# Closing a pair of sequences behind the second down product, and sending its rows one iteration later

## The chip, the cores and the metric

The kernel runs on one core of a Trainium2 chip. A core has five engines, each with its own in-order stream of instructions: TensorE (PE in the profile; PEld is its weight load), VectorE (DVE), ScalarE (ACT), GpSimd (POOL) and SyncE (SP, which here only issues DMAs and reads registers). They wait for each other through semaphores. The metric is the device time of one execution in microseconds, given as the median of several runs. Beside it stands one profiled execution, whose trace has the start and the duration of every instruction.

## The reference: what is computed

The model has two layers on 32 sequences of 128 tokens with 512 features. Each layer adds a feed-forward part, applied to a mixture-of-experts part, to its input:

```python
x = x + ffn0(cond0(x, ...))      # cond0: shared expert + 2 of 8 routed experts
x = x + ffn1(cond1(x, ...))      # cond1: hashed experts;  ffn1: a recurrent scan
```

The change touches only the end of the first line and the entry of the second. `ffn0` chooses one of 8 experts for each whole sequence (its own expert) from the sequence's last token, and then computes for all its tokens

```python
h = gelu(hidden @ w1 + b1)               # 512 -> 1024
reasoned = h @ w2 + b2                   # 1024 -> 512
out = hidden + 0.3 * (reasoned @ Wo + bo)
```

`cond1` first mixes each token with the one before it in its sequence, with two sets of coefficients:

```python
xk = x + (xprev - x) * time_maa_k        # goes to the hashed experts
xr = x + (xprev - x) * time_maa_r        # goes to r = sigmoid(xr @ w_recept.T)
```

The stage that is changed hands on three things for every sequence: the new `x` itself, the rows of `xk`, and the rows of `xr @ w_recept.T`.

## The kernel before, in words

All products are made in a split format: each float32 operand is stored as a rounded high part and the remainder, and a product is three matmuls (high x high, high x low, low x high). The helper `split` makes the two parts with one ScalarE cast and one VectorE subtraction; the helper `mm3` makes the matmuls. In the profile every matmul of a split product therefore has line L64, every cast L56 and every subtraction L57, and one reads by the names of the tiles.

The stage of the sequences' own experts is one loop (line 1115), over `b` from -1 to 32. It is software-pipelined: iteration `b` makes the first products of sequence `b+1`, the second products of sequence `b`, and the closing work of earlier sequences. The sequences were sorted by expert beforehand in two parts (0 to 23 and 24 to 31), so that neighbours mostly share their weights.

- `up(b, half)` (line 981): half of the 512-to-1024 product, 12 matmuls of 512 columns, tile `pu`; ScalarE copies it out as `ue`.
- `bend(b, half)` (line 988): four transposes (tile `pt`), four ScalarE gelus (tile `hf`), then a split into `hb`, which the down product reads.
- `down(b, half)` (line 1000): half of the 1024-to-512 product, 12 matmuls, tile `po`. After half b ScalarE copies the sum out as `ps`.
- `turn_r(b)` (line 1012): four transposes of `ps` (tile `pr`), then four times a ScalarE step and a VectorE step that write the high and low part of `rT`. Each ScalarE step here waits for the VectorE step before it.
- `close(c)` (line 1029) for the pair of sequences `2c` and `2c+1`: 48 matmuls of 256 columns against `Wo` (tile `pb`), then on VectorE the new `x1` (line 1058), the difference `dx` (L1041), `xk` (four instructions, L1043). GpSimd writes the first column of `x1` (L1034); SyncE stores `x1`, two DMAs.
- `fetch_xh(c)` (line 967): two DMAs that load the next pair's addend. `mix_r(c)` (line 1075): four VectorE instructions that turn `dx` into the other mix (L1079), then a split into `xr` (ScalarE cast, VectorE subtraction).
- `send_k(b)` (line 1085): four transposes of `xk` (tile `ptB`), a ScalarE copy into `rows`, one store. `send_v(b)` (line 1095): 12 matmuls of `xr` against `w_recept` (tile `pv`), a ScalarE copy into `r`, one store. `rows` and `r` share two buffers.
- `used()` (line 1110) stands behind each of the four weight products. It holds the split of the next weight of that kind (`split_w`, line 839: two casts and two subtractions of 128 x 1024), inside a branch that ScalarE and VectorE take only if the next sequence has another expert; then GpSimd gathers the weight three places further on. By the casts in the trace the branches are taken for sequences 7, 16, 24 and 27.

The transposes `pt`, `pr` and `ptB` share two PSUM banks (pool `ps_t`), `pb` and `pv` share three.

Within a stretch between two such branches the framework's scheduler may reorder instructions; across a branch no engine's instructions move. So the order of the lines of the loop decides the coarse order on every engine, and the scheduler the fine one.

In the kernel before, a pair is closed in iteration `b = 2c+2` between `up(b+1, "b")` and `down(b, "b")`. Each iteration then ends with `send_k(b-2)` and `send_v(b-2)`: one sequence of the pair in the iteration that closed it, the other in the next.

The stage ends with the last pair and the sends that are left over (lines 1167 to 1176); the expert stage behind it gathers the rows that were sent.

Of the kernel before, what the change touches and what calls it, by code (L numbers as in the profile page):

```python
# [23 lines left out]
NB = 32  # L24
# [21 lines left out]
def tile_kernel(ctx: ExitStack, tc: tile.TileContext, a: dict, out: bass.AP):  # L46
# [7 lines left out]
    def split(hi, lo, src):  # L54

        nc.scalar.copy(hi, src)  # L56
        return nc.vector.tensor_tensor(lo, src, hi.bitcast(F32), ALU.subtract).ins  # L57

    def mm3(ps, left, right, kd, start=True, stop=True):

        last = 3 * kd - 1
        for k in range(kd):
            for n, (hl, hr) in enumerate(((0, 0), (0, 1), (1, 0))):
                done = nc.tensor.matmul(  # L64
                    ps, lhsT=left(hl, k), rhs=right(hr, k),
                    start=start and k + n == 0, stop=stop and 3 * k + n == last,
                )
        return done.ins
# [67 lines left out]
    with ExitStack() as sa:  # L136
# [105 lines left out]
        with ExitStack() as s0:  # L242
# [32 lines left out]
            def rtile(shape, name, dt=F32, tag=None):  # L275
                return rt.tile(shape, dt, name=name, tag=tag or name)
# [33 lines left out]
            down = rtile([P, E0], "down")  # L310
# [525 lines left out]
        def bias_of(kind, b, o):  # L836
            return bcol[b][:, BIAS[kind] * KD + o : BIAS[kind] * KD + o + 1]

        def split_w(i):

            if i < len(todo):
                raw = raws.pop(i)
                kind, b = order[todo[i]]
                if b not in (0, PARTS[0]) and b not in changed:
                    changed[b] = nc.values_load(
                        new_i[0:1, b : b + 1], engines=[nc.scalar.engine, nc.vector.engine],
                        min_val=0, max_val=1,
                    )
                flat = ws[kind].rearrange("p h k n -> p h (k n)")
                with tc.If(changed[b] != 0) if b in changed else nullcontext():  # L850
                    for q in range(2):
                        s = bass.ts(q, KD * D // 2)
                        split(flat[:, 0, s], flat[:, 1, s], raw[:, s])
                fetch_w(i + AHEAD)
# [61 lines left out]
    with ExitStack() as sb:  # L916
# [34 lines left out]
        def rows_of(t, p):  # L951

            return t[bass.ds((seq(p) + where(p)[0] * PARTS[0]) * P, P), :]
# [5 lines left out]
        def fetch_hid(b):  # L959
            if b < NB:  # L960
                hid_raw[b] = lp.tile([P, KD, P], F32, tag="hid", name=f"hidB_{b}")
                nc.sync.dma_start(out=hid_raw[b].rearrange("p k q -> p (k q)"), in_=by_seq(hid_d, b))
# [4 lines left out]
        def fetch_xh(c):  # L967
            if c < NB // PB:
                xs[c] = lp.tile([P, PB, KD, P], F32, tag="x", bufs=1, name=f"xB_{c}")
                for j in range(PB):  # L970
                    nc.sync.dma_start(
                        out=xs[c][:, j].rearrange("p k q -> p (k q)"), in_=by_seq(xh_d, c * PB + j)
                    )

        def split_hid(b):
            if b < NB:
                raw = hid_raw.pop(b)
                hid_hl[b] = lp.tile([P, 2, KD, P], FR, tag="hidhl", name=f"hidhl_{b}")
                split(hid_hl[b][:, 0], hid_hl[b][:, 1], raw)

        def up(b, half):
            w = ws["W1" + half]
            pu = ps_u.tile([P, HF], F32, tag="u", name=f"pu_{b}{half}")
            mm3(pu, lambda h, k: hid_hl[b][:, h, k, :], lambda h, k: w[:, h, k, :], KD)
            ues[b, half] = rp.tile([P, HF], F32, tag="ue", name=f"ue_{b}{half}")
            nc.scalar.copy(ues[b, half], pu)

        def bend(b, half):

            ue = ues.pop((b, half))  # L990
            pt = ps_t.tile([P, KD, P], F32, tag="t", name=f"pt_{b}{half}")
            for f in range(KD):
                nc.tensor.transpose(pt[:, f, :], ue[:, bass.ts(f, P)], ident)
            hf = rp.tile([P, KD, P], F32, tag="hf", name=f"hf_{b}{half}")
            for f in range(KD):
                nc.scalar.activation(hf[:, f, :], pt[:, f, :], AF.Gelu, bias=bias_of("W1" + half, b, f))
            hbs[b, half] = rp.tile([P, 2, KD, P], FR, tag="hb", bufs=3, name=f"hb_{b}{half}")
            split(hbs[b, half][:, 0], hbs[b, half][:, 1], hf)

        def down(b, half):  # L1000
            w, hb = ws["W2" + half], hbs.pop((b, half))
            if half == "a":
                pos[b] = ps_o.tile([P, D], F32, tag="o", name=f"po_{b}")
            mm3(
                pos[b], lambda h, k: hb[:, h, k, :], lambda h, k: w[:, h, k, :], KD,
                half == "a", half == "b",
            )
            if half == "b":
                pss[b] = rp.tile([P, D], F32, tag="ps", bufs=1, name=f"ps_{b}")
                nc.scalar.copy(pss[b], pos.pop(b))  # L1010
# [74 lines left out]
        def send_k(b):  # L1085
            c, j = divmod(b, PB)
            pt = ps_t.tile([P, KD, P], F32, tag="t", name=f"ptB_{b}")
            for k in range(KD):
                nc.tensor.transpose(pt[:, k, :], xks[c][0][:, k, j, :], ident)
            rows = rp.tile([P, D], F32, tag="rows", bufs=2, name=f"rows_{b}")  # L1090
            done = nc.scalar.copy(rows, pt.rearrange("p k q -> p (k q)"))
            nc.sync.dma_start(out=rows_of(xk_d, b), in_=rows)
            return done.ins

        def send_v(b):
            c, j = divmod(b, PB)
            pv = ps_b.tile([P, D], F32, tag="b", name=f"pv_{b}")
            mm3(pv, lambda h, k: xrs[c][:, h, k, j, :], lambda h, k: wrec[:, h, k, :], KD)
            tag = "rows" if b < NB - 6 else ("ue", "hf")[b % 2]
            r = rp.tile([P, D], F32, tag=tag, bufs=2, name=f"r_{b}")  # L1100
            nc.scalar.copy(r, pv)
            nc.sync.dma_start(out=rows_of(v_d, b), in_=r)
# [7 lines left out]
        def used():  # L1110
            nonlocal at
            split_w(at + AHEAD)
            at += 1

        for b in range(-1, NB + 1):
            c, j = divmod(b - 1, PB)
            if b + 1 < NB:
                up(b + 1, "a")
                used()
                split_hid(b + 2)  # L1120
                fetch_hid(b + 3)
            if 0 <= b - 1 < NB:
                r_done = turn_r(b - 1)
            if 0 <= b < NB:
                down(b, "a")
                used()
            if b == -1:
                fetch_xh(0)
            if b == 0:
                wo0 = weight_b("Wo")  # L1130
            if b == 1:
                wrec = weight_b("w_recept")

            late, step = divmod(b - 3, 3)
            if 0 <= late < GB and step == 0:
                get_o(NB - GB + late, cb, 1)
            if 0 <= late < GB and step == 2:
                combine(NB - GB + late, ps_t)
            if late == GB and step == 2:
                policy(PARTS[0], NB, cb, ps_t)  # L1140
            if b + 1 < NB:
                bend(b + 1, "a")
                up(b + 1, "b")
                used()
            if late == GB and step == 2:
                sc.close()
                end_p = sb.enter_context(tc.tile_pool(name="end_p", bufs=1, **kw))
            if b == NB:
                send_v(NB - 6)
            if j == PB - 1 and 0 <= c < NB // PB:  # L1150
                wo_done, k_done = close(c, b == NB)
                fetch_xh(c + 1)
                if c < NB // PB - 2:
                    mix_r(c, bp, "xr")
                elif c == NB // PB - 2:
                    mix_r(c, end_p, "xr")
            if 0 <= b < NB:
                down(b, "b")
                used()
            if b + 1 < NB:  # L1160
                bend(b + 1, "b")
            if 0 <= b - 2 < NB - 2:
                send_k(b - 2)
                if b - 2 < NB - 6:
                    send_v(b - 2)

        with tc.issue_after(wo_done):
            send_v(NB - 5)
# [484 lines left out]
```

## Time and profile before

| | |
|---|---|
| median of 3 runs | 2569.21 us (2566.71 to 2570.12) |
| the profiled execution: its time | 2573.86 us |
| its span, first to last instruction | 2572.1 us |
| mean granted TensorE clock | 0.987 |
| PE busy over the span | 2490.9 us |
| the loop of own experts | about 876 to 1500 us of the span |
| PE busy in 876 to 1500 us | 606.05 us of 624.00 |
| DVE, ACT, POOL busy there | 283.43, 312.22, 176.73 us |

The page of a profile gives busy time by engine; the view of windows gives the same for a stretch of the span; the view of waits tells which instruction sat idle until which other had ended; the timeline lists instructions in order of time, runs of equal ones merged. An engine's idle time matters only where that engine sets the pace, here TensorE.

### The profile page before, as it was taken

What the parts mean: (1) busy time and instruction counts of PE and PEld (TensorE: products, weight loads), DVE (VectorE), ACT (ScalarE), POOL (GpSimd) and SP (SyncE); (2) the same over time, 40 slices, a digit from 0 to 9 for tenths busy, and PEclk for the clock granted to TensorE, in tenths of its full rate; (3) what the DMA queues carried; (4) which work ended last, traced back from release to release, by engine and by line L of the source; (5) the groups of instructions that cost most, each with busy time, mean ns of one, the idle gap of its engine ahead of it and who ended that gap; (6) DMA issues with size and microseconds to landing.
All of it is one profiled execution on the core that took longest, in us unless ns stands there. A gap on an engine that the chain in (4) does not pass through costs nothing. (4 is left out here: it accounts for less than half of the span.)

```text
span 2572.1 us, 37393 instructions
## 1 busy us (share of the span) xinstructions
PE 2490.9 (97%) x13044; PEld 2080.6 (81%) x13044; DVE 1374.6 (53%) x2413; ACT 1103.7 (43%) x2007; POOL 430.1 (17%) x458
## 2 busy tenths in 40 slices
PE   8999999999997999999999999999989999999996
PEld 6788799978786777888887889999978888888885
DVE  7897654557777444445454476667643332333336
ACT  4545533334445545455455466666532221222214
POOL 1000022222222223333222110000010000000003
PEclk9999999999998999999999999999999999999998
DMA  5545544467886333333243287777441111111027
GB/s 179 160 131 173 171 150 155 150 234 243 264 279 221 119 107 112 100 120 107 83 138 114 89 290 236 229 225 220 145 164 43 40 37 37 37 42 45 26 73 267
DMA packets 203486, 370.00 MB, mean 144 GB/s; under 512 B 38624, under 2 KB 73488, under 8 KB 200224
## 3 DMA queue, kind: packets, MB, share of 16 engines
q1 hardware_dynamic: 151872, 263.30, 30.9%
q0 software_dynamic: 36160, 74.90, 10.1%
q10 hardware_dynamic: 15264, 29.37, 3.1%
q8 instruction: 108, 1.77, 0.3%
q14 instruction: 82, 0.67, 0.1%
HBM read 392.81 MB, written 88.13 MB: 187 GB/s over the span
## 5 line engine op out<-in xcount | busy, mean ns | idle before, releaser
L64 PE MATMUL p<-xhl,swu 128*128 128x512 f32 x1536 | 378.5, 399 | 13.9 <-DVE sg L202 7.0
L64 PEld LDWEIGHTS p<-xhl,swu 128*128 128x128 f32 x1536 | 289.6, 191 | 76.3 <-issue 7.7
L57 DVE TENSOR_TENSOR wD<-rawD,wD 128x1024 fp32r<-128x1024 f32 x128 | 156.3, 1228 | 78.8 <-ACT wD L56 78.8
L64 PE MATMUL acc<-swd,as 128*128 128x512 f32 x768 | 192.1, 396 | 2.9 <-DVE as L57 1.8
L64 PEld LDWEIGHTS phD<-xe,wD 128*128 128x128 f32 x1536 | 186.8, 191 | 1.7 <-ACT wD L56 0.5
L64 PE MATMUL phD<-xe,wD 128*128 128x256 f32 x1536 | 187.8, 284 | 0.3 <-DVE hf L1249 0.3
L64 PE MATMUL poD<-wD,hD 128*128 128x512 f32 x768 | 181.9, 393 | 0.0
L64 PEld LDWEIGHTS acc<-swd,as 128*128 128x128 f32 x768 | 143.7, 188 | 38.8 <-DVE as L57 4.5
L64 PEld LDWEIGHTS poD<-wD,hD 128*128 128x128 f32 x768 | 142.1, 188 | 28.8
L56 ACT CAST wD<-rawD 128x1024 fp32r<-128x1024 f32 x128 | 133.2, 1046 | 54.6 <-PE poD L64 49.3
L246 POOL DMA_INDIRECT xg<-in_x_rows_dram,blk_t x71 | 67.8, 955 | 469.3 <-PE ptx L256 264.1
L1335 POOL DMA_INDIRECT y<-res_d,gat_i x32 | 32.4, 1013 | 584.5 <-DVE r L1354 505.2
L64 PE MATMUL pur<-r,xb 128*128 x852 | 118.6, 288 | 1.7 <-ACT xb L56 0.8
L64 PE MATMUL por<-r,hbr 128*128 x426 | 117.4, 409 | 1.9 <-ACT hbr L56 1.5
L56 ACT CAST swu<-swr 128x512 fp32r<-128x512 f32 x128 | 74.8, 619 | 91.5 <-PE p L64 61.3
L57 DVE TENSOR_TENSOR xb<-ptx,xb 128x512 fp32r<-128x512 f32 x71 | 49.0, 691 | 113.2 <-ACT xb L56 113.2
L64 PEld LDWEIGHTS pur<-r,xb 128*128 128x128 f32 x852 | 105.5, 189 | 3.3 <-ACT xb L56 1.3
L64 PE MATMUL pv<-w_recept_hl,xr 128*128 128x512 f32 x384 | 101.9, 411 | 5.9 <-DVE xr L57 5.9
L64 PE MATMUL ps_f<-wf_hl,z 128*128 128x512 f32 x384 | 97.9, 402 | 2.4 <-ACT wf_hl L56 1.7
L64 PE MATMUL ps_c<-wc_hl,z 128*128 128x512 f32 x384 | 96.6, 398 | 0.7 <-ACT z L56 0.7
L64 PE MATMUL poF<-z,wo_hl 128*128 128x512 f32 x384 | 96.7, 399 | 0.0
L64 PEld LDWEIGHTS pb<-rT,Wo_hl 128*128 128x128 f32 x768 | 93.2, 188 | 4.2 <-DVE rT L1023 2.7
(1004 smaller groups left out, 4834.7 us busy)
## 6 DMA issues: line engine op xcount, KB each, us to landing
swr<-in_sw_dram SPq DMA_DIRECT2D x192, 256.0 KB, 3.9
rawD<-in_w_key_dram SPq DMA_DIRECT2D x64, 512.0 KB, 4.1
rawD<-in_w_value_dram SPq DMA_DIRECT2D x64, 512.0 KB, 4.0
o_d<-obr SPq DMA_DIRECT2D x71, 256.0 KB, 2.4
xraw<-in_x_dram SPq DMA_DIRECT2D x32, 256.0 KB, 4.6
rraw<-in_rw_dram SPq DMA_DIRECT2D x32, 256.0 KB, 3.4
xc<-in_x_dram SPq DMA_DIRECT2D x32, 256.0 KB, 4.4
hid_d<-o ACTq DMA_DIRECT2D x32, 256.0 KB, 3.7
```

What stands on the lines that cost most here:

```text
L56: nc.scalar.copy(hi, src)
L57: return nc.vector.tensor_tensor(lo, src, hi.bitcast(F32), ALU.subtract).ins
L64: done = nc.tensor.matmul(ps, lhsT=left(hl, k), rhs=right(hr, k), start=start and k + n == 0, stop=stop and 3 * k + n == last,)
L246: nc.gpsimd.indirect_dma_start(out=xg[i], out_offset=None, in_=a["x_rows"], in_offset=bass.IndirectOffsetOnAxis(ap=blk_t[:, i : i + 1], ax ...
L1335: nc.gpsimd.indirect_dma_start(out=y, out_offset=None, in_=res_d, in_offset=bass.IndirectOffsetOnAxis(ap=gat_i[:, b : b + 1], axis=0),)
```

## The change

Four things move, and nothing is added or removed: the same instructions are issued for every sequence.

- In an even iteration `close`, `fetch_xh` and `mix_r` move from before `down(b, "b")` to the end of the iteration, behind `down(b, "b")` and `bend(b+1, "b")`.
- Even iterations no longer send anything. Both sequences of a pair are sent in the odd iteration that follows.
- There, the two `send_k` stand around `up(b+1, "b")`, behind `bend(b+1, "a")`.
- The two `send_v` stand around `bend(b+1, "b")`, behind `down(b, "b")`.

```diff
             if b + 1 < NB:
                 bend(b + 1, "a")
+
+            pair = b - 3 if b % 2 and 0 <= b - 3 < NB - 2 else None
+            if pair is not None:
+                send_k(pair)
+            if b + 1 < NB:
                 up(b + 1, "b")
                 used()
             if late == GB and step == 2:
                 sc.close()
                 end_p = sb.enter_context(tc.tile_pool(name="end_p", bufs=1, **kw))
+            if pair is not None:
+                send_k(pair + 1)
             if b == NB:
                 send_v(NB - 6)
+            if 0 <= b < NB:
+                down(b, "b")
+                used()
+            if pair is not None and pair < NB - 6:
+                send_v(pair)
+            if b + 1 < NB:
+                bend(b + 1, "b")
+            if pair is not None and pair < NB - 6:
+                send_v(pair + 1)
             if j == PB - 1 and 0 <= c < NB // PB:
                 wo_done, k_done = close(c, b == NB)
                 fetch_xh(c + 1)
...
-            if 0 <= b < NB:
-                down(b, "b")
-                used()
-            if b + 1 < NB:
-                bend(b + 1, "b")
-            if 0 <= b - 2 < NB - 2:
-                send_k(b - 2)
-                if b - 2 < NB - 6:
-                    send_v(b - 2)
```

## The prediction

> **What bounds the kernel now.** I read the head of the page first: TensorE is busy for 97% of the span.
>
> ```profile
> span 2572.1 us, 37393 instructions
> PE 2490.9 (97%) x13044; PEld 2080.6 (81%) x13044; DVE 1374.6 (53%) x2413; ACT 1103.7 (43%) x2007; POOL 430.1 (17%) x458
> ```
>
> So only gaps of TensorE count. Next the waits of PE in the loop, 876 to 1500 us (who waited, for whom, total, times, longest):
>
> ```profile
> PE pv L64 <- DVE xr L57: 5.9, 2, 2.9
> PE ptB L1089 <- DVE xk L1043: 5.2, 3, 2.1
> ...
> PE pb L64 <- DVE rT L1023: 2.5, 1, 2.5
> ```
>
> All three come from tiles that the change gives more time. Third, windows of one pair of iterations, PE alone (length, busy, clock, DMA):
>
> ```profile
> 1235.56:1273.15 37.59, 37.57 (x204) 1.00 0.24 71
> ...
> 1348.32:1390.68 42.36, 39.39 (x203) 0.96 0.45 138
> ```
>
> The usual pair takes 37.59 us with almost no idle time; the second one, where the weights of sequence 27 are exchanged, takes 4.8 us more. Its timeline shows why, first PE:
>
> ```profile
> 1352.69 0.71 PE L64 MATMUL po<-wB_W2a,hb_25a 128*128 128x512 f32 x2
> 1356.35 3.98 PE L64 MATMUL pv<-w_recept_hl,xr 128*128 128x512 f32 x10 [2.95 <-DVE xr L57]
> ```
>
> PE stands 2.95 us, and the next ten matmuls take 3.98 us instead of about 2.4: a reduced clock. VectorE and ScalarE at that time:
>
> ```profile
> 1345.12 0.76 DVE L1058 SCALAR_TENSOR_TENSOR x<-pb,xB 128x256 f32<-128x256 f32 x2 [2.09 <-PE pb L64]
> 1345.98 1.22 DVE L1041 TENSOR_TENSOR dx<-x 128x1024 f32<-128x1024 f32 x1
> 1347.24 1.91 DVE L1043 SCALAR_TENSOR_TENSOR xk<-dx,maa_k_sb,x 128x256 f32<-128x256 f32 x4
> 1349.07 1.67 DVE L1079 SCALAR_TENSOR_TENSOR dx<-dx,maa_r_sb,x 128x256 f32<-128x256 f32 x4
> 1350.71 0.69 DVE L57 TENSOR_TENSOR hb_25b<-hf_25b,hb_25b 128x512 fp32r<-128x512 f32 x1
> 1352.80 2.36 DVE L57 TENSOR_TENSOR wB_W1a<-rawB,wB_W1a 128x1024 fp32r<-128x1024 f32 x2 [1.39 <-ACT wB_W1a L56]
> 1355.07 1.22 DVE L57 TENSOR_TENSOR xr<-dx,xr 128x1024 fp32r<-128x1024 f32 x1
> ```
>
> ```profile
> 1350.77 1.05 ACT L56 CAST xr<-dx 128x1024 fp32r<-128x1024 f32 x1
> 1351.72 1.99 ACT L56 CAST wB_W1a<-rawB 128x1024 fp32r<-128x1024 f32 x2
> ```
>
> From the end of the close (1344.92) the chain x1, dx, xk, second mix ends after 5.82 us, and xr follows; the weight exchange pushes in between.
>
> **What the Trainium skill says.** "PSUM — Partial Sum Buffer", section "Engine vs sequencer instructions": the ScalarE and VectorE queues are strict FIFO. The trace agrees: above, the xr subtraction stands behind the 2.36 us of weight subtractions though its cast had ended at 1351.82. "TensorE: Matmul & The Clock Gate", Part 1: the clock falls to half after an idle window of about 3.4 us that runs freely. Here shorter waits do it: four of 2.06 to 2.95 us were followed by slow matmuls that cost 1.2 to 1.65 us, one of 2.51 us (in iteration 6) was not.
>
> **The change part by part.** Nothing is added or removed, so the sum is over waits. I use the trace's start-to-start times on PE: up 2.79 us, pr 0.36, down 2.89, pt 0.35, seven of twelve matmuls of the second up 1.73. Zero is the end of the close.
>
> *The usual odd iteration.* Before, ptB follows the close after one down product and pt, 3.3 us, so its four transposes wait for single xk pieces, woven into the next up; all losses of that weave above the plain rate are 0.68 us a pair (0.26 + 0.09 + 0.09 + 0.05 + 0.11 + 0.08). After, the order of the changed program is up, pr, down, pt, seven matmuls of up b, ptB: PE gets there at 2.79 + 0.36 + 2.89 + 0.35 + 1.73 = 8.1. xk is ready by about 4.2. But ptB now takes the PSUM bank of pt, so it waits for the gelus, and on ScalarE the order is: first rT step, *xr cast*, branch for W2a, second rT step, gelus. The cast waits for the second mix: 5.87 + 1.05 = 6.92, branch not taken 0.23 (four xk take 1.91 us with such a branch among them and 1.68 in the last pair, without), rT 0.37, four gelus 1.14 less overlaps: 8.5. PE waits 0.4; with 0.1 for one weave that is 0.5 instead of 0.68. Seven such iterations (3, 11, 13, 17, 19, 21, 29): -1.3 us.
>
> *Iterations 5 and 25 (W1a exchanged).* Before they lose 4.84 us and 5.1. After, the two subtractions stand between the xk pieces: second mix ends at 5.82 + 2.3 = 8.1, cast 9.2, branch and rT 9.7, gelus 10.8. PE waits 2.7 from 8.1. In 5 a combine puts another transpose and a ScalarE copy (0.6 us) in place of the gelus: pt waits 10.25 - 7.4 = 2.85. A slow clock costs 1.45; I take two chances in three, 1.0. Together 3.85 + 3.7 against 9.9: -2.3.
>
> *Iteration 6.* Before, pb lost 2.84 us on rT, because VectorE stood 6.59 us on a gathered row. After, the close stands 3.2 us later; I find 0.65 left at the next pt: -2.2.
>
> *Iterations 7 and 27.* Before, the exchange of W2b split the xk chain: 3.98 and 3.99 us. After, that exchange ends before the first x1 is ready (13.1 against 15.4 us after the up product began), so the usual 0.5 remains: -7.0. *Iteration 9*: a combine had delayed xk by 1.4; 0.5 remains: -0.9.
>
> *Iterations 15 and 23 (W2a exchanged).* Before no wait, 0.68. After, the two casts of W2a (1.99 us) stand on ScalarE behind the xr cast and ahead of the gelus: 6.92 + 1.95 = 8.9, rT 9.25, gelus 10.4: PE waits 2.3. Then the second ptB waits for the rows copy, which stands behind a third rT step, and this behind VectorE's W2a (2.36), xr (1.22) and rT: 12.85 against 11.95, 0.9 more. With 1.0 for the clock and 0.1: 4.2 each, +7.0 for both. This is what the change pays.
>
> *The end.* In iteration 31 nothing but pr and one down product stands between close 14 and its ptB: 0.5 for single pieces, 0.4 at pr for the ps copy behind the xr cast, against 0.5 before: +0.6. What follows close 15 is the same on all engines.
>
> *What costs nothing.* Each pair still issues two x1 stores, two xh loads and four stores on SP; the rows stores land in a median of 2.4 us, and a buffer is reused about 6 us later (rows copied near 9.8, r near 16). The bare cover is that gap; if SP were 3 us late, ScalarE would stop at the r copy with the gelus behind it. GpSimd's copy into x1 and its gathers stand further from their uses than before; it waited 83.2 us for xk without PE noticing. If its gather of a changed weight came late, the split and then the up product would wait. The wait of 1.35 us in iteration 14 stays.
>
> Sum: -1.3 - 2.3 - 2.2 - 7.0 - 0.9 + 7.0 + 0.6 = -6.1 us. The profiled execution, 2573.86 us (span 2572.1), would come to about 2568; it lies 4.65 above the median, so the median goes from 2569.2 to 2563.
>
> **The rivals.** *No change that can be told.* A measurement tells about 0.2% here, 5 us. If all four long waits that I leave (5, 15, 23, 25) meet the slow clock, that is +1.8, and a second rows wait in 5 and 25 like that of 15 adds 1.8: -2.5 us, 2567. For it: sizes of 1 us decide, and the clock window's phase is open.
>
> *Slower: ScalarE's order becomes the bound.* The xr cast waits for VectorE with the gelus behind it, and PE needs the bank. If the cast ends later than 6.92, every odd iteration pays in full, 14 times. From 0.8 us later (14 x 0.8 = 11.2) the -6 turns into +5; at 1.2 us it is +11, 2580. For it: the gelus did not stand behind the cast before, and semaphore passages of 0.05 to 0.2 us add up along eight steps. Against it: each duration is taken from this trace, 5.82 repeats in three pairs, and before, after the same chain, the cast began on time.
>
> *TensorE's plain rate.* If the scheduler's waits melt (gelus ahead of the cast in effect), all of 0.68 a pair and the exchanges' losses vanish: about 16 x 0.6 + 24 = 33 less the rest, 2540. Against it: the order on ScalarE is fixed.
>
> **How the numbers follow.** Forecast, 2557 to 2565: 0.47. No change: 0.33. Slower: 0.15. Plain rate: 0.05. The range reaches from 2555 (both clock chances won, the usual wait 0) to 2573, where the usual wait is 1.1 us. Of the forecast a part ends within 5 us, of the second rival a part beyond: faster 0.50, same 0.36, slower 0.14. The likeliest case's own range is 2558 to 2566.
>
> **What would show it.** Right: pairs of 37.4 us where no weight changes; no pv or pb among PE's waits; ptB waiting for ACT hf, about 0.4 us each and 2.3 to 2.7 in 15, 23 and 25. Wrong: ptB waits over 0.8 us in usual iterations, ScalarE waiting for the landing of rows, a wait of close for rT, or 15 and 23 without a gap.

## The result, and the profile after

The changed kernel takes 2561.76 us (median of 20 runs, 2556.24 to 2570.40). The kernel before, run beside it, takes 2573.55 us (20 runs; the 2569.21 us given above were the first three). The ratio is 0.9962, with a 95% interval of 0.9954 to 0.9971. On 2573.55 us that is 9.8 us less (7.5 to 11.8); the two medians themselves lie 11.8 us apart, at the edge of this. The forecast was 6.1 us less, to 2563 us. The absolute time is close partly because the three early runs of the kernel before were low; the difference came out 3.7 us larger than forecast. The profiled execution of after took 2566.27 us and lies 4.5 us above its median, while that of before lies at its median (2573.86). The two traces therefore show a smaller gain, 7.5 us of span. Between traces I compare the loop alone: in the 14 traces of this case the first up product of the loop begins anywhere from 859.7 to 868.9 us, though the code ahead of it is nearly the same in all.

The head of the page of the kernel after:

```profile
span 2564.6 us, 37411 instructions
PE 2484.2 (97%) x13044; PEld 2081.5 (81%) x13044; DVE 1372.3 (54%) x2413; ACT 1101.7 (43%) x2007; POOL 437.8 (17%) x458
```

TensorE is still busy for 97%. The waits of PE in 876 to 1500 us, after the change (who waited, for whom, total, times, longest):

```profile
PE pt_6a L993 <- ACT o L717: 2.4, 1, 2.4
PE pt_15a L993 <- DVEq L850: 2.3, 1, 2.3
...
PE ptB L1089 <- ACT hf_26a L996: 2.3, 1, 2.3
PE ptB L1089 <- ACT hf_16a L996: 1.9, 1, 1.9
...
PE ptB L1089 <- ACT hf_20a L996: 0.2, 1, 0.2
```

The 13.6 us for xr, xk and rT (5.9 + 5.2 + 2.5) are gone. In their place stand four waits of about 2 us. Three of them are for readers on ScalarE. The fourth, pt_15a, stood at 1.1 us before and has doubled; it begins at 1138.12, right behind VectorE's last rT step (end 1138.06). Usual iterations wait 0.2 us.

The windows of one pair of iterations, the same two pairs as before (length, PE busy, ..., clock, DMA, GB/s at the end of the line):

```profile
1231.11:1268.65 37.54, 37.34 (x203) 31.30 (x201) 14.06 (x28) 17.14 (x41) 11.34 (x11) 1.00 0.23 71
1343.51:1384.70 41.19, 38.89 (x202) 32.56 (x201) 23.35 (x36) 24.82 (x49) 11.50 (x11) 0.96 0.36 116
```

The usual pair went from 37.59 to 37.54 us: practically nothing. The pair with an exchange went from 42.36 to 41.19 and still contains a reduced clock. Its timeline after the change, PE first and then ScalarE:

```profile
1349.55 0.60 PE L993 MATMUL pt_26a<-ident,ue_26a 128*128 128x128 f32 x4
1349.91 1.88 PE L64 MATMUL pu_26b<-wB_W1b,hidhl 128*128 128x512 f32 x7
1354.08 0.98 PE L1089 MATMUL ptB<-ident,xk 128*128 128x128 f32 x4 [2.30 <-ACT hf_26a L996]
```

```profile
1347.94 0.38 ACT L1022 ACTIVATE rT<-pr,b 128x128 fp32r<-128x128 f32 x1
1351.46 1.05 ACT L56 CAST xr<-dx 128x1024 fp32r<-128x1024 f32 x1 [3.15 <-DVE dx L1079]
1352.63 0.37 ACT L1022 ACTIVATE rT<-pr,b 128x128 fp32r<-128x128 f32 x1
1352.89 1.14 ACT L996 ACTIVATE hf_26a<-pt_26a,b 128x128 f32<-128x128 f32 x4
```

The order on ScalarE is the one that the prediction wrote down: first rT step, xr cast, second rT step, gelus. The gelus end at 1354.03 and ptB begins at 1354.08.

Where the time went in the two profiled executions, by the start of the first up product of each sequence (after less before, for one iteration):

| iteration | forecast | measured |
|---|---|---|
| 5 | -1.0 | -0.88 |
| 6 | -2.2 | -2.94 |
| 7 | -3.5 | -3.33 |
| 9 | -0.9 | -1.32 |
| 14 | 0 | +2.61 |
| 15 | +3.5 | +3.64 |
| 23 | +3.5 | -0.10 |
| 25 | -1.4 | -1.02 |
| 27 | -3.5 | -3.30 |
| the end, to the last pv | +0.6 | +0.01 |
| all others together | -1.2 | -0.24 |
| sum | -6.1 | -6.87 |

Eight rows agree within 0.8 us or so. Two are wrong by more than 2.5 us, with opposite signs: iterations 14 and 23. In the row "all others together", 0.68 us lost in iteration 0, while the pipeline starts, is set against 0.92 us gained in usual iterations.

### The profile page after: what moved, and what is told of

It is laid out like the page before. It is cut to its first block, busy times and chain, and to the rows that moved or that the text cites. A ratio compares the mean times of both kernels' runs of the same rounds, so it can differ in the third digit from the quotient of the medians.

```text
span 2564.6 us, 37411 instructions
## 1 busy us (share of the span) xinstructions
PE 2484.2 (97%) x13044; PEld 2081.5 (81%) x13044; DVE 1372.3 (54%) x2413; ACT 1101.7 (43%) x2007; POOL 437.8 (17%) x458
## 5 line engine op out<-in xcount | busy, mean ns | idle before, releaser
L695 POOL DMA_INDIRECT o<-o_d,s_i x64 | 74.8, 1169 | 145.7 <-DVE o L711 46.1
L64 PE MATMUL ps_i<-wi_hl,z 128*128 128x512 f32 x384 | 95.3, 395 | 0.8 <-DVE wi_hl L57 0.8
```

The source lines that it names most:

```text
L64: done = nc.tensor.matmul(ps, lhsT=left(hl, k), rhs=right(hr, k), start=start and k + n == 0, stop=stop and 3 * k + n == last,)
L695: nc.gpsimd.indirect_dma_start(out=o[n], out_offset=None, in_=o_d, in_offset=bass.IndirectOffsetOnAxis(ap=idx[:, b : b + 1], axis=0),)
```

## The experiments

The theory after the result: what the change gains are waits at weight exchanges, where the sends asked for xk and xr before these were ready; what it pays are waits for a PSUM bank whose last reader, mostly on ScalarE, is late. All times below are compared with the kernel before, run beside each.

**Where the gain lies.** In both kernels the exchange of the weights of sequences 7, 16 and 27 is left out (those sequences then compute with the weights of the sequence before them):

```diff
-            nc.vector.tensor_scalar(new_i[:, b0:b1], same, -1.0, 1.0, ALU.mult, ALU.add)
+            nc.vector.tensor_scalar(new_i[:, b0:b1], same, 0.0, 0.0, ALU.mult, ALU.add)
```

> The kernel before, with the weights of sequences 7, 16 and 27 never exchanged: the branch that holds their splits is not taken, so these sequences compute with the weights of the sequence before (sequence 24, which has no branch, still exchanges). Theory: the losses at 5, 7, 25 and 27 (4.8, 4.0, 5.1 and 4.0 us) vanish, so about -17 us against before (-13 to -20), ratio about 0.9934. A rival that puts the gain of the change into usual iterations expects the same here but differs in the next kernel.

> The kernel after with the same branches never taken (the weights of sequences 7, 16 and 27 left out as in the kernel before it). Theory (nearly all that the change gains and loses lies at weight exchanges): the waits of 14, 15 and 25 vanish; what is left of the change against the kernel before without exchanges is iteration 6 and 9 (a combine, not an exchange), -2 to -4.5 us, of which 5's wait for the output of a combine may take back up to 3. So -1 to -4.5 us against it. Rival (the gain lies in the weave of usual iterations): the whole -10 us remains, at least -7.

Measured: 2554.94 us without exchanges before (ratio 0.9928, 0.9910 to 0.9946), 2551.64 us after (0.9912, 0.9895 to 0.9928). So 3.3 us of difference are left, with intervals that overlap. The traces are sharper: over the loop the two differ by 1.3 us to the last pv, of which iteration 9 has 1.7, and a usual pair 0.0 to 0.4 in one direction or the other. The gain does lie at the exchanges. One part of my expectation was wrong: I had counted the wait of iteration 6 for rT as a combine's. Without exchanges it is not there in either kernel.

```profile
PE ptB L1089 <- DVE xk L1043: 1.4, 1, 1.4
```

This is all that the kernel before waits for in iterations 1 to 31 once the exchanges are out. It is the wait of iteration 9.

**Which half of the change.** The sends stay late; the close goes back ahead of the second down product:

```diff
+            if j == PB - 1 and 0 <= c < NB // PB:
+                wo_done, k_done = close(c, b == NB)
+                fetch_xh(c + 1)
...
             if 0 <= b < NB:
                 down(b, "b")
                 used()
...
-            if j == PB - 1 and 0 <= c < NB // PB:
-                wo_done, k_done = close(c, b == NB)
-                fetch_xh(c + 1)
...
```

> The sends stay one iteration later, but close, fetch_xh and mix_r go back before the second down product of the even iteration. Theory (the gain is waits that went away because what the sends need is ready earlier than they ask; the new waits of iterations 5, 15 and 25 come from the xr cast standing ahead of the gelus): here the chain from the close to the gelus has a down product more, so ptB waits no longer in 15 and 25 and pt_6a no longer in 5, the gain of 7 and 27 stays, the pb wait of iteration 6 (2.5 us) is back, iteration 14 still loses about 2.6. Against before: 5 and 25 give -9.9, 7 and 27 -8, iteration 9 -1.4, 14 +2.6, so about -16 us (-11 to -20), ratio about 0.9937. Rival (it is the close behind the down product that gains, not the later sends): no better than -3 us, ratio 0.999 or more.

Measured: 2569.51 us, ratio 0.9980 (0.9970 to 0.9990), about 5 us less than before. Neither expectation fits: I had forecast 16 less. The waits of PE in this kernel:

```profile
PE ptB L1089 <- DVE rT L1023: 10.0, 6, 3.1
...
PE pt_6a L993 <- DVE rT L1023: 3.2, 1, 3.2
```

xk is ready long before here, so the scheduler puts ptB three matmuls earlier, behind four matmuls of the up product instead of seven. There it takes the bank of pr, and pr is held until VectorE has done the last step of rT. Iteration 25 on VectorE:

```profile
1352.76 2.36 DVE L57 TENSOR_TENSOR wB_W1a<-rawB,wB_W1a 128x1024 fp32r<-128x1024 f32 x2 [1.46 <-ACT wB_W1a L56]
1355.04 1.22 DVE L57 TENSOR_TENSOR xr<-dx,xr 128x1024 fp32r<-128x1024 f32 x1
1356.18 0.35 DVE L1023 SCALAR_TENSOR_TENSOR rT<-pr,b,rT 128x128 fp32r<-128x128 f32 x1
```

The four rT steps alternate between the two engines and end at 1358.88; ptB starts at 1358.94, 3.13 us late. So the xr cast ahead of the gelus cannot be the whole cause of such waits: here it ran at 1350.73, well out of the way, and the wait is longer than in the kernel after. The other half alone, a late close with the sends where they were, was not run.

**The xr cast.** First as a move of lines only: the split of xr comes out of `mix_r` and stands behind the second `send_k`.

```diff
-            xrs[c] = pool.tile([P, 2, KD, PB, P], FR, tag=tag, name=f"xr_{c}")
-            split(xrs[c][:, 0], xrs[c][:, 1], dx)
...
             if pair is not None:
                 send_k(pair + 1)
+                split_r(pair // PB, bp if pair < NB - 4 else end_p, "xr")
```

> As after, but the split of the second mix (cast and subtraction) is taken out of mix_r and stands behind the second send_k in the odd iteration; only the pairs of the loop, the last one excepted. Theory (the xr cast ahead of the gelus makes the waits of 5, 15 and 25): ptB no longer waits for the gelus in usual iterations (0.2 us each now), 2 to 3 us of each of the waits in 5, 15 and 25 go and with them the slow clock behind them, so about 8 us faster than after (5 to 12), ratio to before about 0.993. Rival (these waits come from VectorE's weight subtractions and rT steps and the cast only stands in the same row): less than 2 us faster than after. Third way: pv waits for the late xr, over 1 us in usual iterations, and the kernel is slower than after.

Measured: 2563.50 us, ratio 0.9962 (0.9952 to 0.9972), the same as after. The trace shows why it tells nothing about the cast: the scheduler put it back in its old place, between the first two rT steps, and the whole order in the loop is that of after except for one place in iteration 9. It is in effect a repetition of after, and useful as one: its profiled execution gained 2.46 us in iteration 5 and 2.54 in iteration 25, where that of after gained 0.88 and 1.02, because the clock stayed full behind the same waits of 2.4 and 2.3 us.

Second, with an order given explicitly: the cast of xr is issued behind the last gelu of the same iteration.

```diff
             if pair is not None:
                 send_k(pair + 1)
+                with tc.issue_after(gelus[b + 1]) if b + 1 < NB else nullcontext():
+                    split_r(pair // PB, bp if pair < NB - 4 else end_p, "xr")
```

> As after, with ScalarE's cast of xr ordered behind the last gelu of the same iteration (the second try, with an explicit order on ScalarE, of the experiment in which the scheduler had put the cast back where it was). First theory (the cast ahead of the gelus makes the waits): ptB waits 0 in usual iterations and the waits of 15 and 25 shrink by more than 2 us each, about 8 us faster than after. Second theory (the gelus also stand behind the second rT step, and this behind VectorE's first one, which comes after the weight's subtractions and the second mix): the wait in 25 falls by about 1 us, to 1.3, that in 5 alike; in 15 the casts of W2a stay ahead, so it falls by about 1 too; short enough that the slow clock stays away, so 3 to 6 us faster than after.

Measured: 2564.39 us, ratio 0.9958 (0.9942 to 0.9974): no difference to after that can be told. The 0.2 us of usual iterations went, the wait in 25 fell only from 2.3 to 1.9 us, that in 5 from 2.4 to 1.8, and that in 15 rose from 1.9 to 3.0. The loop of this trace is 7.3 us shorter than that of after, 2.8 of it in iteration 14, where pt_15a waits 1.1 us as before the change (more on this below); the times show no such gain. ScalarE in iteration 15 of this kernel:

```profile
1161.07 0.37 ACT L998 ACTIVATE hf_16a<-pt_16a,b 128x128 f32<-128x128 f32 x1
1162.91 0.37 ACT L1026 ACTIVATE rT<-pr,b 128x128 fp32r<-128x128 f32 x1 [1.48 <-DVE rT L1027]
1163.18 0.88 ACT L998 ACTIVATE hf_16a<-pt_16a,b 128x128 f32<-128x128 f32 x3
```

Without the cast the scheduler drew a third rT step in between the gelus, and that step waits for VectorE, which subtracts W2a meanwhile. The second theory is nearer, but its sizes failed as well. The wait is not one instruction in the wrong place. Gelus and rT steps stand in one row on ScalarE, every rT step hangs on VectorE, and on VectorE stand the exchange's subtractions.

**The bank.** The Trainium skill counts eight PSUM banks in a partition ("PSUM — Partial Sum Buffer", section "Specifications (TRN2)"). No run here shows that number, but the pools of this loop add up to it: two for pu, one for po, two shared by pt, pr, ptB and the transposes of the combine (pth), three shared by pb and pv. So ptB cannot get a bank of its own. Here it moves to the last group:

```diff
-            pt = ps_t.tile([P, KD, P], F32, tag="t", name=f"ptB_{b}")
+            pt = ps_b.tile([P, KD, P], F32, tag="b", name=f"ptB_{b}")
```

> As after, but the transposes of xk (ptB) take one of the three PSUM banks of pb and pv instead of one of the two that they shared with pt and pr. Theory (ptB waits in 15 and 25, and 0.2 us in usual iterations, because its bank is held until ScalarE has come to the gelus): both waits go with their slow clock, 4.1 and 3.9 us, and 7 times 0.2; iterations 5 and 14, where pt waits, stay. About 9 us faster than after (7 to 11), ratio to before about 0.9927. Rival (ScalarE and VectorE are late as such, and the wait only moves on to pv, to the next down product or to the copies of rows): less than 3 us faster than after.

Measured: 2553.24 us, ratio 0.9917 (0.9900 to 0.9934). That is 21 us less than before and 11.6 us less than after, if the two ratios are set against each other. Iteration 15 costs 4.0 us less than in after, and 25 costs 4.1 less (expected 4.1 and 3.9); the sum is somewhat above the 9 that I had put down. The timeline of iteration 25, PE and ScalarE:

```profile
1347.72 0.60 PE L993 MATMUL pt_26a<-ident,ue_26a 128*128 128x128 f32 x4
1348.16 0.60 PE L1089 MATMUL ptB<-ident,xk 128*128 128x128 f32 x4
```

```profile
1351.05 1.14 ACT L996 ACTIVATE hf_26a<-pt_26a,b 128x128 f32<-128x128 f32 x4
```

The gelus still begin 3.3 us after the start of pt_26a, as in after (1352.89 - 1349.55). Nothing on ScalarE became faster. Only nobody on TensorE asks for that bank any more, and the wait did not move on to pv or the next down product. This settles the cause of the waits in 15 and 25: the shared bank.

The same with the close ahead of the down product, and the same in the kernel before:

> As the first experiment (sends late, close ahead of the second down product) with ptB in the banks of pb and pv. Theory (the close may stand at either place; what counts is that the sends come later and that ptB does not wait for a bank): the ten us that ptB and the slow clock behind it lost in the first experiment go, about 15 us less than there, ratio to before about 0.9925. Rival (the place behind the down product is what gains): at most 5 us less than the first experiment, ratio 0.996 or more.

> The kernel before, with ptB in the banks of pb and pv. Theory (before the change ptB waits for the data of xk and pv for xr, not for a bank; the bank became the limit only when the sends came later): no difference, -1.5 to +1.5 us, ratio 0.9994 to 1.0006. Rival (the shared bank costs by itself, whatever is sent when): the same 10 us as behind the change, ratio 0.996.

Measured: 2557.92 us, ratio 0.9935 (0.9918 to 0.9951), and 2571.84 us, ratio 0.9999 (0.9989 to 1.0010). The first gained 11.6 us on its counterpart instead of 15; pt_6a and pt_15a still wait 3.2 us each there. Together with the others:

| sends | close | ptB shares with | ratio to before |
|---|---|---|---|
| early | early | pt, pr | 1 |
| early | early | pb, pv | 0.9999 |
| late | early | pt, pr | 0.9980 |
| late | early | pb, pv | 0.9935 |
| late | late | pt, pr | 0.9962 |
| late | late | pb, pv | 0.9917 |

The bank is worth nothing while the sends are early, for then ptB waits for data, and 0.45% (11.6 us) at either place of the close once they are late. The late close is worth about 0.18% either way (4.6 us), which is at the edge of what two intervals can tell. The larger part of the idea is thus the later send, and more than half of its worth was lost to the bank.

**Two stores in one iteration.** Close late as in after, but one sequence sent per iteration, each one iteration later than before the change:

```diff
-            pair = b - 3 if b % 2 and 0 <= b - 3 < NB - 2 else None
+            pair = b - 3 if 0 <= b - 3 < NB - 2 else None
...
-            if pair is not None:
-                send_k(pair + 1)
...
-            if pair is not None and pair < NB - 6:
-                send_v(pair + 1)
```

> As after, but one sequence of the pair is sent in the odd iteration and the other in the following even one, as before, only one iteration later than before. Theory (iteration 14 loses because the two stores of rows of one iteration stand in line on SP, so the r copy on ScalarE and with it the casts for sequence 16 come late): the wait of pt_15a goes from 2.3 back to 1.1 or less, its slow clock goes, 15 loses 0.3 less; 25 and 5 as in after. About 3 us faster than after (2 to 5). Rival (the chain would be late all the same): no difference to after in iteration 14. What could spoil it: ptB in even iterations waits for the bank of pr.

Measured: 2574.02 us, ratio 1.0001 (0.9989 to 1.0013): the whole gain is lost, though the part in question came out as expected. Over iterations 13 and 14 (from the first up product of sequence 14 to that of 16) after loses 2.76 us against before, this kernel 0.10. The trace of after, SP in iteration 13 and ScalarE behind it:

```profile
1119.42 5.87 SPq L1092 DMA_DIRECT2D xk_d<-rows  x2
```

```profile
1131.52 0.59 ACT L1101 COPY r<-pv 128x512 f32<-128x512 f32 x1 [3.28 <-DMA xk_d<-rows]
1132.00 2.00 ACT L56 CAST wB_W1a<-rawB 128x1024 fp32r<-128x1024 f32 x2
```

The second store of rows is issued 5.5 us after the first (1124.9 against 1119.4), because SP waits for the first to land. The copy of the second r then waits 3.28 us for that store, as the two share a buffer, and the casts of W1a for sequence 16 queue up behind it. That is the order on one engine that the Trainium skill states ("PSUM — Partial Sum Buffer", section "Engine vs sequencer instructions"), and the trace agrees. With one store per iteration no copy of r waits for a landing, pt_15a waits 1.2 us instead of 2.3, and the slow clock behind it is gone.

Two stores in one iteration do not always cost this. In the kernel with the cast behind the gelus both stand in iteration 13 too, and the DMA engines are nearly as busy (a share of 0.67 and then 0.72 from 1124 to 1133 us, against 0.71 and 0.82 in after). There the second store is issued 3.3 us after the first, the copy of the second r waits only for PE, and iteration 14 loses nothing:

```profile
1124.12 3.69 SPq L1101 DMA_DIRECT2D xk_d<-rows  x2
1133.04 0.59 ACT L1110 COPY r<-pv 128x512 f32<-128x512 f32 x1 [0.89 <-PE pv L64]
```

Why these stores landed sooner is not shown. It also takes an exchange behind the copy: in the kernel after without exchanges the same copy waits 3.42 us for a landing, and iteration 14 is only 0.25 us longer than in its counterpart.

What spoiled this kernel is mainly one wait in iteration 6, on VectorE and then on PE (a second one of the same kind, 1.65 us, stands in iteration 12):

```profile
985.32 0.75 DVE L712 SCALAR_TENSOR_TENSOR o<-o,g,o 128x512 f32<-128x512 f32 x1 [5.88 <-DMA o<-o_d,s_i]
```

```profile
991.16 1.12 PE L1089 MATMUL ptB<-ident,xk 128*128 128x128 f32 x4 [7.16 <-DVE rT L1023]
```

VectorE stands on a gathered row, the rT steps stand behind it, and the second sequence's ptB, which now comes in this iteration, takes pr's bank. Hence the next kernel, with ptB in the banks of pb and pv as well:

> ptB in the banks of pb and pv, and one sequence sent per iteration instead of two in the odd one. Theory (two stores of rows in one iteration stand in line on SP, which costs iteration 14 about 2.7; what spoiled one send per iteration by itself was only that ptB waited 7.2 us for the bank of pr in iteration 6): against the same kernel with both sends in the odd iteration, iteration 14 gains 2.7 and iteration 6 loses nothing, so about 2550.5 us, ratio to before about 0.9907 (0.9900 to 0.9915). Rival (the 7 us that VectorE stands on a gathered row in iteration 6 hit the next user of a bank instead, pt of the second half): +5 there, 2556 us, ratio 0.993.

Measured: 2551.82 us, ratio 0.9918 (0.9904 to 0.9932). Against 0.9917 with both sends in one iteration the times show no difference, and 2.7 us could not be told between two such intervals. The traces show it at its place: pt_15a waits 1.3 us instead of 2.5, without a slow clock, and iterations 13 and 14 together take 2.8 us less. The 7.16 us of iteration 6 are gone.

**Iteration 23.** The weights of sequence 24 are exchanged too, yet 23 lost nothing. In the kernel this exchange has no branch, although the description of the kernel before lists 24 among the branches. Here it gets one:

```diff
-                if b not in (0, PARTS[0]) and b not in changed:
+                if b != 0 and b not in changed:
```

> As after, but the exchange of the weights of sequence 24 stands in a branch like those of 7, 16 and 27 (its condition is true). Theory (iteration 23 escaped the wait of 15 only because its casts of W2a stood in no branch, so that the scheduler could spread them around the gelus): iteration 23 now loses what 15 loses, ptB waiting about 1.9 us for the gelus, with the slow clock about 3.5 us slower than after (2 to 4.5), ratio to before about 0.9975. Rival (it escaped because the two parts differ in something else, such as when the weight arrives): no difference to after, ratio 0.9962.

Measured: 2566.62 us, ratio 0.9976 (0.9969 to 0.9984), which is 3.6 us above after; the two intervals (0.9971 ends the one, 0.9969 begins the other) only just touch. PE in iteration 23 of this kernel:

```profile
1317.06 0.66 PE L1089 MATMUL ptB<-ident,xk 128*128 128x128 f32 x4 [1.87 <-ACT hf_24a L996]
...
1319.49 0.66 PE L1089 MATMUL ptB<-ident,xk 128*128 128x128 f32 x4 [0.59 <-ACT rows L1091]
```

These are the two waits that I had forecast for 15 and 23, and the clock stays full behind them in this trace. In after, ScalarE did one of the two W2a casts in the time when it stood still ahead of the xr cast, and the other behind the gelus:

```profile
1311.02 1.05 ACT L56 CAST wB_W2a<-rawB 128x1024 fp32r<-128x1024 f32 x1 [0.98 <-PE po L64]
1312.03 1.05 ACT L56 CAST xr<-dx 128x1024 fp32r<-128x1024 f32 x1
...
1313.24 1.13 ACT L996 ACTIVATE hf_24a<-pt_24a,b 128x128 f32<-128x128 f32 x4
1314.24 1.07 ACT L56 CAST wB_W2a<-rawB 128x1024 fp32r<-128x1024 f32 x1
```

**The last waits.** If the waits of pt are also for banks, the combine's transposes (pth) can leave that pair of banks too. This comes on top of one send per iteration and ptB in the banks of pb and pv:

```diff
-                combine(NB - GB + late, ps_t)
+                combine(NB - GB + late, ps_b, "b")
```

> As the kernel with one send per iteration and ptB in the banks of pb and pv, with the transposes of the combine (pth) there too, so that pt and pr have their two banks alone. Theory (every wait of pt and ptB left in the loop is for a bank whose reader is late on ScalarE): pt_6a loses its 2.5 us in iteration 5, pt_15a its 1.1, pt_12a its 0.4; about 4 us less, 2546.5 us, ratio to before about 0.989. Rival (the reader is late as such: then the gelus, and with them the next use of the bank, wait all the same): less than 1 us.

Measured: 2547.84 us, ratio 0.9900 (0.9885 to 0.9915), the fastest of all: 25.7 us less than before and 4.0 less than the kernel that it builds on, as expected, though their intervals still overlap. In the trace nothing of the old waits is left from 890 to 1470 us. The view of PE's waits there has one line:

```profile
PE pt_7b L993 <- ACT ue_7b L986: 0.7, 1, 0.7
```

## Why the prediction was right, and where it was wrong

*Direction and mechanism.* Right, with gaps. The waits of xr, xk and rT are gone, the exchanges of 7 and 27 gave 6.6 us where 7.0 were forecast, and without exchanges before and after differ by 1.3 us in the trace. The usual iteration waits 0.2 us, where 0.4 were forecast. Of the signs that I had named for being wrong, two did appear: ScalarE waits for the landing of rows (three times, 8.6 us together), and 23 has no gap.

*"Iterations 15 and 23".* The loss in 15 was forecast to 0.14 us (3.5 and 3.64), but this is partly luck. The terms 2.3, 0.9, 1.0 and 0.1 add up to 4.3, where I wrote 4.2, and they did not come out one by one: PE waits 1.87 and 0.24 us instead of 2.3 and 0.9, and the slow clock came in full, which I had put at 1.0 us. For 23 the step failed: I took for granted that both exchanges stand in a branch. The code says that sequence 24 has none, and without one the casts went around the gelus. With a branch iterations 22 and 23 together lose 3.3 us more than in after by the trace (23 alone 2.7), and the ratio says 3.6.

*"What costs nothing".* The step that failed for iteration 14. I named the cover (a buffer is reused about 6 us later, a store lands in a median of 2.4) and what would happen if SP were late, but took the median landing for every store and overlooked that the second store is issued only after the first has landed. In iteration 13 the DMA engines are busy (a share of 0.71 to 0.82 from 1119 to 1131 us), SP waits 5.0 us for the first landing, the second store lands about 6.6 us after its issue (the copy of r that waits for it begins at 1131.52), and the two together exceed the cover by 3.3 us. The price is 2.6 us with the slow clock. Half a sentence of the forecast had it: "if SP were 3 us late, ScalarE would stop at the r copy". I gave it no share of the sum.

*"Iterations 5 and 25" and the usual one: the cause.* The walk along ScalarE gave the right times, since it contained every instruction in its order. The name that I gave to the cause, the xr cast with the gelus behind it, holds only in part: with the cast out of the way these waits fell by 0.4 to 0.6 us, and 15 grew. What makes a late gelu a wait of TensorE is that ptB shares pt's bank. The prediction said so in half a sentence and then put its attention on the cast.

*"Iteration 6".* Forecast 2.2 less, measured 2.9. My reading that VectorE's wait on the gathered row alone makes this loss was wrong: without exchanges VectorE still stands 4.07 us on the gathered row, and PE does not wait there. The trace of before shows what else it took. The subtractions of W2a for sequence 7 stand ahead of the last rT step, for which the close waits:

```profile
991.08 2.36 DVE L57 TENSOR_TENSOR wB_W2a<-rawB,wB_W2a 128x1024 fp32r<-128x1024 f32 x2 [1.37 <-ACT wB_W2a L56]
993.36 0.34 DVE L1023 SCALAR_TENSOR_TENSOR rT<-pr,b,rT 128x128 fp32r<-128x128 f32 x1
```

```profile
993.76 4.77 PE L64 MATMUL pb<-rT,Wo_hl 128*128 128x256 f32 x38 [2.51 <-DVE rT L1023]
```

*The size.* The misses at 14 (+2.6) and 23 (-3.6) nearly cancel, so a good sum is no proof of its terms. The rest of the distance to 9.8 us cannot be pinned to a step. In the profiled execution of after all four long waits were followed by the slow clock, where I had taken two chances in three. The near-repetition escaped it in iterations 5 and 25, and its loop gained 10.3 us instead of 6.9. Which waits meet the slow clock changes from one execution to the next, as the last section shows.

*The rivals.* "No change" is excluded by the interval. "ScalarE's order becomes the bound" did not occur: the usual wait is 0.2 us. "TensorE's plain rate" was put at 2540 and is nearly what the kernel with the banks set apart reaches. I had reckoned that it would need the gelus ahead of the cast. It needed other banks for ptB and pth, and one send per iteration.

## What to carry to other kernels

When a consumer is moved later so that its data is ready, look next at the buffer that it writes: from then on it waits for the last reader of that buffer, and a spare bank in another pool may be worth as much as the move (here 11.6 us, against nothing before the move). When stores are collected into one iteration, count the second one from the landing of the first, at the load of that stretch and not by the median (here the second was issued 5.5 us after the first in one trace and 3.3 in another). Read from the code which conditional work really has a branch, for around a branch the scheduler's freedom ends.

## What the runs showed of the hardware

The clock fell behind waits of about 2 us in some executions and not in others. A wait of 1.87 us in iteration 15 of after was followed by a granted clock of 0.67 over the next 5 us, one of 1.92 us in iteration 25 of the kernel with the cast behind the gelus by 1.00; within one execution of the kernel with ptB in pb's banks, 2.48 us (iteration 5) by 1.00 and 2.5 us (iteration 14) by 0.69. The columns are length, busy times of PE, PEld, DVE, ACT and POOL, then the clock:

```profile
1161.80:1167.00 5.20, 4.96 (x19) 3.69 (x20) 3.19 (x7) 3.50 (x7) 3.15 (x4) 0.67 0.19 63
```

```profile
1356.30:1361.00 4.70, 4.62 (x24) 3.90 (x25) 3.77 (x5) 4.70 (x9) 1.42 (x1) 1.00 0.17 57
```

The clock's own records in the 14 traces say more. Within the loop every stretch at half clock lasts 3.41, 6.83 or 10.24 us, which is one, two or three times 3.41, and within one trace these stretches begin whole multiples of 3.41 us apart (in after at 965.14, 1139.22, 1163.12 and 1354.26 us: 51, 7 and 56 steps). On this grid a wait counts by how much of it falls into one step. Below are two steps of iteration 5 of after, then three of iteration 5 of the kernel with ptB in pb's banks, where the wait is as long:

```profile
961.73:965.14 3.41, 0.96 (x7) 0.69 (x6) 2.56 (x7) 1.93 (x4) 1.69 (x2) 1.00 0.03 6
965.14:968.55 3.41, 3.41 (x10) 2.61 (x9) 1.83 (x7) 3.27 (x9) 1.62 (x3) 0.50 0.58 182
```

```profile
964.93:968.35 3.42, 2.72 (x16) 1.96 (x15) 3.35 (x8) 0.29 (x1) 1.28 (x1) 1.00 0.72 232
968.35:971.76 3.41, 1.63 (x9) 1.44 (x10) 2.63 (x7) 3.19 (x8) 2.19 (x3) 1.00 0.24 90
971.76:975.17 3.41, 3.41 (x18) 2.78 (x17) 1.47 (x3) 3.18 (x7) 2.94 (x4) 1.00 0.77 230
```

In after the whole wait of 2.45 us lies in one step (PE busy for 0.96 us of 3.41), and the next step runs at half clock. In the other kernel the wait of 2.48 us is split over two steps (0.70 and 1.78 us idle), and the clock stays full. From 885 to 1470 us of all 14 traces, the clock fell after each of the 19 steps at full clock with 2.05 us or more of idle time, after none of those with 1.78 or less, and after five of the ten between 1.84 and 1.94. So the waits of 1.87 and 1.92 us above lie at the border, and a longer one can be harmless: 3.2 us in iteration 5 of the kernel with the early close were split into 1.28 and 1.91, and the clock stayed full.

The grid fits the free-running window of about 3.4 us of which the Trainium skill tells ("TensorE: Matmul & The Clock Gate", Part 1). The skill lets the clock fall after a whole idle window; here somewhat more than half of one was enough. What a fall costs shows between after and its near-repetition, which have the same waits: with it iteration 5 took 1.6 us longer and iteration 25 1.5 us.

SP waits on a semaphore between two stores to one tensor. The skill says that sharing a DMA engine does not put a DMA behind an earlier one on which it depends, and that the issuing engine has to wait for the first one's semaphore ("DMA: Bandwidth & Descriptors", section "Two DMAs through the same engine are not ordered"). Whether these two stores depend on each other is not shown here. The trace shows the price of the wait, 5.0 us at a DMA share of 0.71 to 0.82, where the median landing of these stores in the kernel before was 2.4 us.
